# Dealing the side work of an eight-block group anew in a hybrid attention and state-space kernel

## The chip, the cores and the metric

The kernel runs on one core of one Trainium2 chip. The metric is the device time of one execution in microseconds: the median of repeated runs on the chip. The engines are named as in the profile: PE (TensorE, matrix products; PEld its weight loads), DVE (VectorE), ACT (ScalarE), POOL (GpSimd) and SP (the queue that issues the DMAs).

## The reference, cut to what matters

A layer of four parts on x of 4 x 256 rows and 512 columns: attention, a gated feed-forward, a state-space mixer, the feed-forward again. The change touches the mixer alone:

```
proj = layernorm(x) @ in_proj_w.T            # gate 8192 | x 8192, B 1024, C 1024 | dt 128
xBC  = silu(conv1d(xBC, 4 taps) + conv_b)    # each channel for itself, causal
y    = ssd(x, A, B, C, D, dt)                # 128 heads of 64, 8 groups; scores C.B^T times decay
g    = y * silu(gate)
g    = g * rsqrt(mean(g*g over a group's 1024 channels) + eps) * norm_w
x    = x + g @ out_w.T                       # 8192 channels back to 512
```

The state-space sum is computed as attention: within each sequence, the scores C·Bᵀ of a group are multiplied by every head's decay matrix and its step sizes, and then by x.

## The kernel before, in words

All matrix products of weights are made from split operands: a float32 matrix becomes a high part (ACT copies it to the float32r type) and a low part (DVE or POOL subtracts; `split`, L105 to L108), and `mm3` (L110 to L117) adds three products of 128x512 for each of four slices of the inner dimension. A projection of 128 channels for all 1024 rows is thus 24 matmuls of 128x512, in two halves of 12.

The mixer's 8192 channels are 64 blocks of 128 (two heads each), in eight groups of eight (NB = 64, GB = 8, G = 8). The function `block(i, ...)` (L1175) emits one block; `gi` is its place in the group, 0 to 7, `g` the group:

- x is projected (L1187), convolved (`conv`, L961: a bias and first tap on ACT, L964, three taps on DVE, L971, SiLU on ACT, L975) and later transposed on PE and multiplied by the step sizes (`turned`, L1022: `trx`, then `xd` on DVE).
- the gate is projected (L1208) and goes through SiLU on ACT into `gt` (L1210). A projection's PSUM comes from a pool of two (`pp`), so each waits until the one two before it has been read.
- the decay matrices of its two heads are built from DMA'd rows `r` (L996): clipped differences on DVE (L1004), a causal mask on POOL (L1008, affine select), exponentials on ACT (L1013 to L1016), and a product with the group's masked scores on DVE (L1020). Result: `em`.
- one block later, `inner_products` (L1160) makes the head products on PE (`pyy`, L1044), adds the skip and gates on DVE (L1054, L1057), stores the block to DRAM (`spill`, L1059) and adds its squares on POOL (L1067).

Beside this, each group has side work, dealt over its blocks:

- B and C of the next group: a projection and a convolution each, emitted at the end of blocks 5 and 6 (`NEXT`, L36 and L1218). In block 0 of the next group, `scores` (L978) turns them into the masked scores `gm`, eight small matmuls for each half of two projections. The convolved B and C share a tag of three buffers, `gb`, with the gated blocks.
- the out product of the group before: eight row tiles of 128 (`outer`, L1150), each 24 matmuls of 128x512 (`pog`) and one DVE addition to x (L1115). `PER` (L1174) says how many tiles each block takes: two in block 2, one each in 1 and 3 to 7. The gated blocks are recalled from DRAM at the end of the block before (`recall`, L1097, two halves a tile, two landing buffers `gr`, three split pairs `gh`), split on ACT and DVE.
- the out weights: eight loads of 256 KB a group (`out_weights`, L1073), each scaled by norm_w into a high part on ACT (L1079) and a low part on DVE (L1080). There are eight buffers, so the weights of a group can be written only after the last out product of the group before. Four are emitted in block 7 ahead of its gate, four at its end.

In blocks 0 and 1 (`late`, L1190) the head products of the block before, and the out tiles, are placed between the halves of the gate projection; in the other blocks the first out tile, the head products and the other out tiles stand between x and gate.

The next weights are fetched and split ahead: a projection prepares those of the next two in the order of the list `order` (`prepare`, L813, called at L1129 and L1130). The split's low part is made on POOL for the first 18 of them, on DVE for the rest (L819). The same `order` fixes how the weights lie in DRAM (L1303).

The framework schedules the instructions: each engine's order is fixed when the program is built, by priorities and a model of the engines, and need not be the written order. PE is the exception from group 1 on, where it keeps the written order (`manual_schedule`, L1233). Loads marked `keep_in_program_order` also stay where they are written.

After block 63 come the last head products (L1236), the out product of group 7 tile by tile with the second feed-forward, and the stores.

Of the kernel before, what the change touches and what calls it, by code (L numbers as in the profile page):

```python
# [27 lines left out]
H, PD, N, G = 128, 64, 128, 8  # L28
INTER = H * PD
NB = INTER // P  # L30
GB = NB // G
# [1 line left out]
FH = (NCL + C) // 2  # L33
EPS = 1e-5

NEXT = {5: "b", 6: "c"}  # L36


COLS = {}
# [40 lines left out]
def hybrid_kernel(  # L80
# [6 lines left out]
    nc = tc.nc  # L87
# [17 lines left out]
    def split(hl, v, engine=nc.vector):  # L105

        nc.scalar.copy(hl[0], v)  # L107
        engine.tensor_tensor(hl[1], v, hl[0].bitcast(F32), ALU.subtract)  # L108
# [677 lines left out]
    def mixer(feed, later):  # L786
        with ExitStack() as es, ExitStack() as inner:
# [17 lines left out]
            raws, pieces = {}, {}  # L805
            xs = [w1.tile([P, KC, NT], F32R, name=f"mx{i}") for i in range(2)]

            def fetch(i):
                if i < NW and i not in raws:
                    raws[i] = pw.tile([P, KC, P], F32, name="wr", tag="wr", bufs=3)  # L810
                    load(raws[i], win[i])

            def prepare(i):  # L813

                for n in range(i, i + 3):
                    fetch(n)
                if i < NW and i not in pieces:
                    pieces[i] = [pw.tile([P, KC, P], F32R, name=f"w{j}", tag=f"w{j}") for j in range(2)]
                    split(pieces[i], raws.pop(i), nc.gpsimd if i < 18 else nc.vector)  # L819

            def project(w, pp, cols):
                mm3(pp[:, cols], [[v[:, k, :] for v in w] for k in range(KC)],
# [155 lines left out]
            def scores(bt, ct):  # L978

                gm = p2.tile([P, B, 3, P], F32, name="gm", tag="gm", bufs=1)  # L980
                yield gm
                for b in range(B):
                    pg = ps.tile([P, 3, P], F32, name="pg", tag="m")
                    k0, k1 = bt[:, b * L : b * L + P], bt[:, b * L + P : (b + 1) * L]
                    q1 = ct[:, b * L + P : (b + 1) * L]
                    nc.tensor.matmul(
                        pg[:, 0:2, :].rearrange("p s i -> p (s i)"), k0, ct[:, b * L : (b + 1) * L],
                        start=True, stop=True,
                    )
                    nc.tensor.matmul(pg[:, 2, :], k1, q1, start=True, stop=True)  # L990
                    nc.vector.tensor_tensor(gm[:, b], pg, tri.rearrange("p (s i) -> p s i", s=3), ALU.mult)
                    yield

            def rows(h):
                r = p2.tile([P, NT], F32, name="r", tag="r", bufs=2)
                load(r, cumd[h : h + 1, :].to_broadcast([P, NT]))  # L996
                return r
# [40 lines left out]
            def product(xd, es2):  # L1038
                py = ps_y.tile([P, B, L], F32, name="pyy", tag="pyy")
                for b in range(B):  # L1040
                    for k in range(2):
                        for hh in range(2):
                            d = slice(hh * PD, (hh + 1) * PD)
                            nc.tensor.matmul(  # L1044
                                py[d, b, k * P :], xd[:, 2 * b + k, d],
                                es2[hh][:, b, 2 * k : 2 if k == 0 else 3, :].rearrange("p s i -> p (s i)"),
                                start=(k == 0), stop=(k == 1),
                            )
                return py

            def gated(n, x2, gt, py, sq):

                gb = po_.tile([P, NT], F32, name="gb", tag="gb", bufs=3)
                nc.vector.scalar_tensor_tensor(  # L1054
                    gb, x2, dh[:, n : n + 1], py.rearrange("p b t -> p (b t)"), ALU.mult, ALU.add
                )
                nc.vector.tensor_tensor(gb, gb, gt, ALU.mult)  # L1057
                if n < NB - 1:
                    load(spill[(n // GB) % 2][n % GB], gb)  # L1059
                else:  # L1060
                    last.append(gb)
                if sq is None:
                    sq = p2.tile([P, NT], F32, name="sq", tag="sq")
                    nc.scalar.activation(sq, gb, AF.Square)
                else:
                    nc.scalar.activation(x2, gb, AF.Square)  # L1066
                    (nc.gpsimd if n < NB - 1 else nc.vector).tensor_tensor(sq, sq, x2, ALU.add)  # L1067
                return sq
# [4 lines left out]
            def out_weights(g, k):  # L1073

                r = po_.tile([P, C], F32, name="wor", tag="wor", bufs=2)
                tc.keep_in_program_order(load(r, wout[g * GB + k]))
                n = g * GB + k
                w = [po_.tile([P, C], F32R, name=f"wo{j}", tag=f"wo{j}", bufs=GB) for j in range(2)]
                nc.scalar.activation(w[0], r, AF.Copy, scale=nw_s[:, n : n + 1])  # L1079
                nc.vector.scalar_tensor_tensor(  # L1080
                    w[1], r, nw_s[:, n : n + 1], w[0].bitcast(F32), ALU.mult, ALU.subtract
                )
                return w
# [36 lines left out]
            order = [("b", 0), ("c", 0)]  # L1120
            for n in range(NB):
                order += [("x", n), ("g", n)]
                if n % GB in NEXT and n // GB + 1 < G:
                    order.append((NEXT[n % GB], n // GB + 1))
            at = {v: i for i, v in enumerate(order)}
# [34 lines left out]
            def inner_products(m):  # L1160
                px2, gt, xd, em = stage.pop(m)
                py = product(xd, em)
                sqs[m // GB] = gated(m, px2, gt, py, sqs.get(m // GB))
# [7 lines left out]
            rr = {h: rows(h) for h in range(2)}  # L1171
            stage, sqs, wos, rgs, todo = {}, {}, {}, {}, []
            recalled = []
            PER = {1: 1, 2: 2, 3: 1, 4: 1, 5: 1, 6: 1, 7: 1}  # L1174
            def block(i, scoring, gm):  # L1175
                g, gi = divmod(i, GB)
                if gi == 0 and g:
                    scoring = scores(group["b"], group["c"])
                    gm = next(scoring)
                    todo.extend((g - 1, t) for t in range(TT))  # L1180

                def scored():

                    for _ in range(2 if gi == 0 and g else 0):
                        next(scoring)

                x2 = conv(projected("x", i, scored), i, "x2", 2)  # L1187


                late = gi < 2 and g > 0  # L1190
                if not late:
                    if recalled:
                        outer()
                    if i:
                        inner_products(i - 1)
                    while recalled:
                        outer()
                if gi == 7:
                    wos.setdefault(g, []).extend(out_weights(g, k) for k in range(4))

                def between():
                    scored()
                    if late:
                        inner_products(i - 1)
                        while recalled:
                            outer()

                pp = projected("g", i, between)  # L1208
                gt = p2.tile([P, NT], F32, name="gt", tag="gt", bufs=1)
                nc.scalar.activation(gt, pp, AF.Silu)  # L1210
                em = []
                for h in (2 * i, 2 * i + 1):
                    with tc.issue_after(silus[2]) if i == 0 else ExitStack():
                        em.append(differences(h, rr.pop(h)))
                    if h + 2 < H:
                        rr[h + 2] = rows(h + 2)
                xd = turned(i, x2)
                if gi in NEXT and g + 1 < G:  # L1218
                    convolved(NEXT[gi], g + 1)
                for e in em:  # L1220
                    weighted(e, gm)
                stage[i] = (x2, gt, xd, em)
                for _ in range(PER.get(gi + 1, 0)):
                    if todo:
                        q, t = todo.pop(0)
                        recalled.append((q, t, [recall(q, t, half) for half in range(2)]))
                if gi == 7:
                    wos[g].extend(out_weights(g, k) for k in range(4, 8))
                return scoring, gm

            for i in range(GB):
# [1 line left out]
            with tc.manual_schedule(engines={nc.tensor.engine}):  # L1233
                for i in range(GB, NB):
                    scoring, gm = block(i, scoring, gm)
            inner_products(NB - 1)  # L1236
            es_p.close()
            ps_o = pool("m_o", 4, space=PSUM, **freed)
            pos = {}
# [51 lines left out]
def arrange(inputs):  # L1291
# [12 lines left out]
    for n in range(NB):  # L1304
        order += [NB + n, n]
        g, gi = divmod(n, GB)
        if g + 1 < G and gi in NEXT:
            order.append(2 * NB + (0 if NEXT[gi] == "b" else G) + g + 1)
    blocks = wi[: (2 * NB + 2 * G) * P].reshape(-1, P, KC, P)[order]
# [48 lines left out]
```

## Time and profile before

| | us |
|---|---|
| median of 3 runs | 1892.4 (1890.96 to 1893.69) |
| profiled execution | 1894.86 |
| its span | 1893.1 |
| PE idle, 430 to 545 us (blocks 1 to 7 of group 0) | 3.7 |
| PE idle, 545 to 1800 us (groups 1 to 7) | 20.2 |
| PE idle, 1798 to 1893 us (the end) | 12.8 |

The granted TensorE clock was 0.986 over the span. "Busy" of PE is modelled from pipelined matmuls: a 128x512 matmul is shown with 390 ns, while the next starts 227 ns after it. The other engines' durations are real. A line of the timeline has start (us), duration (us), engine, line, operation, output and inputs, and a count; a bracket gives idle time ahead and what ended it. A line of waits reads: who, for whom, us in total, times, longest.

The windows used below run from one block's gate SiLU (L1210) to the next. In groups 1 to 6 such a window is 19.2 to 20.5 us where one out tile stands in it, about 24 us with B or C besides, 29 to 30 us in block 2 with its two tiles.

### The profile page before, as it was taken

The numbers are of one execution on the slowest core, as the hardware profiler recorded it, in microseconds if no ns is written. First come the engines' busy times: TensorE is split into PE (matmuls) and PEld (weight loads), VectorE is DVE, ScalarE is ACT, GpSimd is POOL, SyncE is SP. The second block draws the span as 40 slices with busy tenths as digits, with TensorE's granted clock in tenths as the row PEclk, the third lists the DMA queues.
The fourth block names the chain that finished last, engine by engine and source line by source line (L and its number), as shares of the span: only waits on it lengthen the run. The fifth ranks groups of instructions, "written<-read, shape, count | busy, mean of one in ns | idle before, by whom it ended". The sixth has DMA issues, their size and how long they took to land.

```text
span 1893.1 us, 29893 instructions
## 1 busy us (share of the span) xinstructions
PE 1812.1 (96%) x10706; PEld 1454.0 (77%) x10706; DVE 1488.3 (79%) x2304; ACT 1479.3 (78%) x2897; POOL 396.4 (21%) x393
## 2 busy tenths in 40 slices
PE   8999988899999999999999999999999999999997
PEld 6777767677777887878778877887887778777876
DVE  5566667788998788878887888778888878887767
ACT  5666675379988888978988888889788978798754
POOL 6322230014411111111212112111211212111100
PEclk8999999899999999999999999999999999999999
DMA  4000000134545445544554445445545544454241
GB/s 143 1 1 1 22 15 16 34 98 157 190 163 177 143 148 163 176 151 145 172 164 148 150 151 173 159 146 164 161 150 167 162 151 145 164 169 152 95 141 49
DMA packets 152773, 240.35 MB, mean 127 GB/s; under 512 B 12464, under 2 KB 77616, under 8 KB 152624
## 3 DMA queue, kind: packets, MB, share of 16 engines
q1 hardware_dynamic: 152624, 238.44, 39.0%
q8 instruction: 84, 1.38, 0.3%
q14 instruction: 65, 0.53, 0.1%
HBM read 202.75 MB, written 35.65 MB: 126 GB/s over the span
## 4 chain that ended last, share of the span: by engine, by line
ACT 34%; PE 25%; DVE 23%; issue 10%; DMA 6%; POOL 2%; SPq 0%; ACTq 0%; DVEq 0%; POOLq 0%
DVE acc L971 9%; ACT em L1013 4%; ACT em L1016 3%; ACT L1210 3%; ACT L1013 3%; ACT em L1014 2%; PE pp L115 2%; PE pp L116 2%; PE pp L117 2%; DVE gh L108 2%; ACT L1016 2%; ACT gt L1210 2%; ACT acc L964 2%; DMA gr<-spill 2%; ACT e L477 2%
## 5 line engine op out<-in xcount | busy, mean ns | idle before, releaser
L115 PE MATMUL pp<-mx,w 128*128 128x512 f32 (+1 forms) x1160 | 464.7, 401 | 10.1 <-ACT gt L1210 7.4
L117 PE MATMUL pp<-mx,w 128*128 128x512 f32 (+1 forms) x1160 | 452.1, 390 | 0.0
L116 PE MATMUL pp<-mx,w 128*128 128x512 f32 (+1 forms) x1160 | 451.9, 390 | 0.0
L1020 DVE TENSOR_TENSOR em<-em,gm 128x1536 f32<-128x1536 f32 x128 | 243.1, 1900 | 110.3 <-ACT em L1016 104.7
L971 DVE SCALAR_TENSOR_TENSOR acc<-pp,cw_s,acc 128x1012 f32<-128x1012 f32 (+2 forms) x240 | 303.7, 1270 | 32.5 <-ACT acc L964 29.1
L1008 POOL TENSOR_SCALAR_AFFINE_SELECT r<-r 128x512 f32<-128x512 f32 x128 | 103.4, 807 | 797.3 <-DMA r<-cumd 648.3
L115 PEld LDWEIGHTS pp<-mx,w 128*128 128x128 f32 x1160 | 218.5, 188 | 64.2 <-ACT gt L1210 11.4
L117 PEld LDWEIGHTS pp<-mx,w 128*128 128x128 f32 x1160 | 218.4, 188 | 46.6 <-issue 0.7
L116 PEld LDWEIGHTS pp<-mx,w 128*128 128x128 f32 x1160 | 218.9, 189 | 40.6 <-issue 0.6
L1067 POOL TENSOR_TENSOR sq<-sq,acc 128x1024 f32<-128x1024 f32 x55 | 151.7, 2759 | 306.3 <-ACT acc L1066 306.3
L115 PE MATMUL pog<-wo,gh 128*128 128x512 f32 x512 | 202.3, 395 | 3.2 <-DVE xd L1030 1.1
L117 PE MATMUL pog<-wo,gh 128*128 128x512 f32 x512 | 200.2, 391 | 2.5 <-DVE gh L108 2.5
L116 PE MATMUL pog<-wo,gh 128*128 128x512 f32 x512 | 199.8, 390 | 0.3 <-DVE wo L1080 0.3
L1044 PE MATMUL pyy<-em,xd 128*64 128x128 f32 (+1 forms) x2048 | 183.7, 329 | 1.3 <-DVE em L1020 1.0
L1013 ACT ACTIVATE em<-r,col_t 128x128 f32<-128x128 f32 x512 | 169.0, 390 | 9.4 <-PE pyy L1044 8.6
L1044 PEld LDWEIGHTS pyy<-em,xd 128*64 128x64 f32 x2048 | 130.1, 137 | 59.9 <-issue 18.0
L1016 ACT ACTIVATE em<-r,col_t 128x128 f32<-128x128 f32 x512 | 170.9, 390 | 0.5
L975 ACT ACT_TABLE_LOAD x65 | 83.4, 1283 | 85.3 <-DVE acc L971 85.0
L1004 DVE TENSOR_SCALAR em<-r,col_t 128x128 f32<-128x128 f32 x512 | 138.0, 324 | 7.0 <-DMA r<-cumd 5.1
L108 DVE TENSOR_TENSOR w<-wr,w 128x512 fp32r<-128x512 f32 x126 | 104.8, 831 | 34.9 <-ACT w L107 32.8
L477 ACT ACTIVATE e<-sc,nmx 128x256 f32<-128x256 f32 (+1 forms) x256 | 104.0, 441 | 21.1 <-DVE nmx L471 21.0
L115 PEld LDWEIGHTS pog<-wo,gh 128*128 128x128 f32 x512 | 96.1, 188 | 27.3 <-DVE xd L1030 2.7
(290 smaller groups left out, 3316.3 us busy)
## 6 DMA issues: line engine op xcount, KB each, us to landing
wr<-in_win_dram SPq DMA_DIRECT2D x287, 256.0 KB, 2.8
r<-cumd SPq DMA_DIRECT2D x128, 512.0 KB, 4.1
spill<-gb SPq DMA_DIRECT2D x63, 512.0 KB, 2.8
gr<-spill SPq DMA_DIRECT2D x120, 256.0 KB, 3.0
wor<-in_wout_dram SPq DMA_DIRECT2D x64, 256.0 KB, 3.2
out_dram<-x SPq DMA_DIRECT2D x8, 256.0 KB, 2.3
x<-in_x_dram SPq DMA_DIRECT2D x1, 1536.0 KB, 8.8
gr<-spill SPq DMA_DIRECT2D x8, 192.0 KB, 2.5
```

Source lines behind the costliest of these rows:

```text
L108: engine.tensor_tensor(hl[1], v, hl[0].bitcast(F32), ALU.subtract)
L115: nc.tensor.matmul(o, lh, rh, start=(first and k == 0), stop=False)
L116: nc.tensor.matmul(o, lh, rl, start=False, stop=False)
L117: nc.tensor.matmul(o, ll, rh, start=False, stop=(last and k == n - 1))
L477: nc.scalar.activation(es_[c][:, 2 * j + pr, :], sc[:, j, :], AF.Exp, bias=nm[:, j : j + 1], accum_out=rs[:, c, h : h + 1],)
L971: nc.vector.scalar_tensor_tensor(av[:, :, d:], pv[:, :, : L - d], cw_s[:, ch, tap : tap + 1], av[:, :, d:], ALU.mult, ALU.add,)
L1004: nc.vector.tensor_scalar(e[:, b, 2, :], rv[:, b, 1, :], col_t[:, h, b, 1:2], 0.0, ALU.subtract, ALU.min,)
L1013: nc.scalar.activation(e[:, b, 1, :], rv[:, b, 1, :], AF.Exp, bias=col_t[:, h, b, 2:3])
L1016: nc.scalar.activation(e[:, b, 0, :], rv[:, b, 0, :], AF.Exp, bias=col_t[:, h, b, 0:1])
L1020: nc.vector.tensor_tensor(e, e, gm, ALU.mult)
L1044: nc.tensor.matmul(py[d, b, k * P :], xd[:, 2 * b + k, d], es2[hh][:, b, 2 * k : 2 if k == 0 else 3, :].rearrange("p s i -> p (s i)"), sta ...
L1067: (nc.gpsimd if n < NB - 1 else nc.vector).tensor_tensor(sq, sq, x2, ALU.add)
```

## The change

Six edits, all in how the side work is dealt:

```
-NEXT = {5: "b", 6: "c"}
+NEXT = {3: "b", 4: "c"}
...
-                    split(pieces[i], raws.pop(i), nc.gpsimd if i < 18 else nc.vector)
+                    split(pieces[i], raws.pop(i), nc.gpsimd if i < 18 or order[i][1] % GB in (7, 0) else nc.vector)
...
-            PER = {1: 1, 2: 2, 3: 1, 4: 1, 5: 1, 6: 1, 7: 1}
+            PER = {1: 1, 2: 2, 3: 1, 4: 1, 5: 2, 6: 1}
...
-                late = gi < 2 and g > 0
+                late = gi in (7, 0, 1) and g > 0
...
-                if gi == 7:
-                    wos.setdefault(g, []).extend(out_weights(g, k) for k in range(4))
+                if gi == 6:
+                    wos.setdefault(g, []).extend(out_weights(g, k) for k in range(3))
...
                 if gi == 7:
-                    wos[g].extend(out_weights(g, k) for k in range(4, 8))
+                    wos[g].extend(out_weights(g, k) for k in range(3, 6))
+                if gi == 0 and g:
+                    wos[g - 1].extend(out_weights(g - 1, k) for k in range(6, 8))
                 return scoring, gm
...
             inner_products(NB - 1)
+            wos[G - 1].extend(out_weights(G - 1, k) for k in range(6, 8))
```

B and C of the next group come behind blocks 3 and 4. The eight out tiles are spread over blocks 1 to 6, two in blocks 2 and 5, none in 7. Block 7's head products move between the halves of its gate projection. The out weights are emitted in three parts: three in block 6 ahead of its gate, three at the end of block 7, two at the end of block 0 of the next group (of the last group: after its last head products). And the low parts of the x and gate weights of blocks 7 and 0 of every group are made on POOL; for B and C, the index is the group's number, so those of group 7 go to POOL too.

The number of instructions and of bytes is the same, but for the engine of these splits.

## The prediction

> **What bounds the kernel now.** I read the page first, then TensorE's waits in the group loop, then busy time in windows (whole loop; group boundaries; single blocks), last the ACT, DVE and POOL timelines at one boundary.
>
> ```profile
> span 1893.1 us, 29893 instructions
> ...
> PE 1812.1 (96%) x10706; PEld 1454.0 (77%) x10706; DVE 1488.3 (79%) x2304; ACT 1479.3 (78%) x2897; POOL 396.4 (21%) x393
> ```
>
> TensorE is busy for 96% of the span. The Trainium skill ("Perfetto Trace Analysis", Identifying the Most-Contended Engine) warns that matmul busy time says little and to take the weight loads' share: 77%, some 23% of room. The trace decides otherwise: in the timeline 128x512 matmuls start every 0.227 us for whole stretches, behind weight loads of 0.19 us, so the room is not there. What can be won is TensorE's idle time:
>
> ```profile
> 430.00:545.00 115.00, 111.31 (x627) 86.32 (x622) 107.66 (x132) 108.67 (x194) 48.28 (x32) 1.00 0.52 170
> 545.00:1800.00 1255.00, 1234.76 (x6774) 992.59 (x6776) 1027.54 (x1369) 1057.34 (x1785) 222.76 (x159) 1.00 0.48 156
> ```
>
> (Columns: us, busy PE, PEld, DVE, ACT, POOL, granted clock, DMA.) 3.7 us idle in group 0 and 20.2 in groups 1 to 7: 24 us in all. Where it lies, by seven windows from one group's last gate SiLU to that of block 1 of the next:
>
> ```profile
> 1268.50:1311.00 42.50, 40.65 (x236) 32.72 (x235) 36.67 (x49) 37.96 (x59) 6.36 (x4) 1.00 0.52 166
> ...
> sum 299.30, PE 283.91 PEld 227.56 DVE 257.59 ACT 266.65 POOL 49.16; mean PE 40.56 PEld 32.51 DVE 36.80 ACT 38.09 POOL 7.02
> ```
>
> 299.30 - 283.91 = 15.4 us, two thirds of the 24, lie at the seven boundaries, 2.2 us each. TensorE's waits name the causes:
>
> ```profile
> PE pp L115 <- ACT gt L1210: 7.4, 8, 1.1
> PE trx L1027 <- ACT acc L975: 5.6, 7, 1.3
> PE pog L117 <- DVE gh L108: 2.5, 6, 0.5
> ```
>
> Block 0's transposes wait for the convolved x (its SiLU), the next x projection for the PSUM that block 0's gate SiLU frees. Both are late because ACT does this in block 0:
>
> ```profile
> 1269.45 1.32 ACT L1079 ACTIVATE wo<-wor,nw_s 128x512 fp32r<-128x512 f32 x2
> ...
> 1275.95 1.19 ACT L964 ACTIVATE acc<-pp,cb_s,cw_s 128x1024 f32<-128x1024 f32 x1
> ...
> 1284.11 1.06 ACT L975 ACTIVATE acc<-acc 128x1024 f32<-128x1024 f32 x1
> 1285.08 1.36 ACT L1079 ACTIVATE wo<-wor,nw_s 128x512 fp32r<-128x512 f32 x2
> ...
> 1291.81 1.02 ACT L1210 ACTIVATE gt<-pp 128x1024 f32<-128x1024 f32 x1
> ```
>
> All eight out weights run between 1269.4 and 1286.4, although half are written ahead of block 7's gate: they fall on block 0, the one block with no out product.
>
> **Part 1: loads of the two light blocks.** After the change block 7 has no out product (24 x 0.227 = 5.4 us less on TensorE) and no C projection behind block 6. It is then like a block of group 0, whose splits are on POOL:
>
> ```profile
> 470.30:484.30 14.00, 14.00 (x82) 10.84 (x81) 13.96 (x18) 13.51 (x27) 7.57 (x5) 1.00 0.57 192
> 484.30:498.90 14.60, 14.60 (x85) 11.29 (x84) 14.17 (x18) 13.70 (x27) 7.91 (x6) 1.00 0.61 200
> ...
> 1244.20:1268.50 24.30, 24.30 (x132) 19.68 (x131) 19.46 (x26) 19.02 (x32) 3.66 (x3) 1.00 0.47 151
> 1268.50:1286.30 17.80, 17.05 (x103) 13.77 (x102) 14.30 (x18) 15.28 (x26) 1.27 (x2) 1.00 0.66 204
> ```
>
> Such a block takes TensorE 14.0 to 14.6 us, with DVE and ACT nearly full and no wait: good news and a warning. DVE of block 7 now: 19.46, less C's convolution and split (3 x 1.27 + 0.69) and the tile's add (0.74), is 14.2 for a bare block. Now: block 7 fits (19.5 in 24.3); block 0 needs 14.2 + 4 x 0.55 (masked scores) + 8 x 0.77 (weights) = 22.5 against 17.05 of TensorE work: 5.5 us behind, of which 2.2 become TensorE waits and 3.3 are absorbed. After: block 7 needs 14.2 - 2 x 0.69 (splits to POOL) + 3 x 0.77 = 15.1 against 14.6; block 0 14.2 + 2.2 + 3 x 0.77 = 18.7 against 17.05; together 2.2 us behind, less than the 3.3 absorbed. Weights 6 and 7 (1.5 us of DVE, 1.4 of ACT) come behind block 0's gate, in block 1 with its out product, and are needed there only after x, half the gate and the block's product. ACT drops five weights (5 x 0.71) ahead of block 0's gate, so its 1.1 us wait goes too. I leave 0.3 us per boundary: 7 x 0.3 - 15.4 = -13.3 us (ends: -15.4, and 0 if the weights bunch again).
>
> **Part 2: a new wait in block 7.** With no out product, from the end of x to the transposes TensorE has only the gate projection and the product: 5.6 + 2.8 = 8.4 us (now 14). In that time ACT and DVE must do bias, three taps, table load and SiLU: in group 0's light blocks 8.2 us (bias at 489.77, SiLU over at 497.9), in block 0 above 9.2 behind a start 1.1 late, in block 4 9.6 behind 3.8. So 0 to 5 us a group. I take 0.5: order and load are group 0's, plus some of three weights. 7 x 0.5 = +3.5. The product's move between the gate's halves (late) costs TensorE nothing and gives the decay products 2.8 us more; without that, they would be due 5.7 us after block 6's transposes, about when they are ready now (1180.65, 5.5 after 1175.2).
>
> **Part 3: splits to POOL.** Four a group (x and gate of blocks 7 and 0), and B and C of group 7 by their index. The Trainium skill ("SBUF — State Buffer", Who interferes with whom) speaks against it: DVE operations with two SBUF inputs and POOL lock one port pair, and the later blocks wholly. The trace, POOL first, then DVE:
>
> ```profile
> 474.99 3.98 POOL L108 TENSOR_TENSOR w<-wr,w 128x512 fp32r<-128x512 f32 x2 [0.75 <-ACT w L107]
> ```
> ```profile
> 443.14 4.50 DVE L1020 TENSOR_TENSOR em<-em,gm 128x1536 f32<-128x1536 f32 x2
> ...
> 474.83 1.75 DVE L1020 TENSOR_TENSOR em<-em,gm 128x1536 f32<-128x1536 f32 x1
> ```
>
> A split takes 2.0 us there. At 474.8 DVE lost nothing beside it; at 443.1, beside two, 4.50 - 2 x 1.75 = 1.0. By the rule four splits block up to 8 us of DVE and save 2.8, and the backlog of 2.2 would exceed 3.3; by the rows they block 0 to 2 and save 2.8. I take the rows, with the gain in part 1. POOL's queue: a split can stand behind an affine select that waits for its rows' DMA; group 0 has the same queue and no wait for it, and a split is called for two projections (over 10 us) ahead.
>
> **Part 4: heavier blocks 3 to 5.** B and C behind 3 and 4, two tiles in 5. DVE in blocks 3 and 4 is 15 to 16 of 20 us; plus 4.5 against 5.4 of TensorE it still fits. B and C hold two of three gb buffers for two blocks more; a gated block gives the third back after its spill (2.8 us), so 0, at most 2.8 a block if the cover goes. Two tiles recalled together need four gh pairs with three there: SP then waits on gr behind DVE, and spills, rows and weights queue behind it. Block 2 does this already, with waits of 0.5 us six times on the late DVE; that shrinks with the backlog and comes back once in block 5. I put the two at 0 (-2.5 to +3.5).
>
> **Part 5: ends.** In group 0 blocks 6 and 7 both become light, with three weights in each: +0.7 (0 to +3). In the last group the weights come earlier; TensorE now waits 1.4 us for them after 1800 (1.1 on ACT, 0.3 on DVE). Two remain late, hidden under four tiles' first halves: -1.2 (0 to -1.5).
>
> Sum: -13.3 + 3.5 + 0.7 - 1.2 = -10.3 us. The profiled execution took 1894.9 us (span 1893.1 and 1.8 around it), 2.5 above the median of the runs; applied to the median, 1892.4 - 10.3 = 1882.
>
> **Rivals.** (a) All waits go: block 7 runs as group 0's light blocks do, 0 there and 0 at the boundary: -15.4 - 2.5 - 1.2 = -19: 1873, and 1867 were all 24 us of the loop to go. For it: the 14.0 us rows. Against it: DVE full before any weight is added. (b) Slower: the x chain of block 7 takes the place of the wait removed. At block 4's 3.8 + 9.6 against 8.4 it costs 5.0 a group, 7 x 5.0 - 13.8 = +21: 1913; at 3 us, +7: 1900. It decides from about 2.0 us a group. For it: ACT starts most convolutions late, and DVE, in order, puts other work between the taps. Against: those blocks' transposes aren't due earlier. (c) The backlog only moves: ACT and DVE still run the weights in one burst in block 0, since operations are not placed where they are written (now they ran 10 us later), or POOL blocks DVE as the rule says. Then the change doesn't do what it says, and gains at most the tail: 1891.
>
> **How the numbers follow.** Likeliest 0.53 (1874 to 1888); (a) 0.13; (b) 0.18, half of it under 1900; (c) 0.16. A measurement tells about 0.2% from no change, 3.8 us. Faster: 0.53 + 0.13 = 0.66; same, (c): 0.16; slower, (b): 0.18. The range, 1868 to 1897, covers all but half of (b) and a tenth at both edges.
>
> **What would show it.** Right: weight scalings in three places, no wait of the transposes in block 0, boundary windows with under 0.6 us of idle TensorE, that of blocks 6 to 7 short by 5 to 11 us and those of 3 to 5 longer. Wrong: transposes of block 7 waiting over 2 us on the SiLU (b); the eight weights still in one run, or DVE's two-input operations stretched beside POOL's splits (c); a new wait on gh in block 5.

## The result, and the profile after

The changed kernel takes 1892.4 us (median of 12 runs, 1889.28 to 1894.44), the kernel before 1891.3 (12 runs beside them). The ratio is 1.0009, with a 95% interval of 0.9999 to 1.002: no difference that these runs can tell. The profiled execution took 1893.5 us, and these are its span, its busy times, and the windows that the prediction used for its idle time (us, busy PE, PEld, DVE, ACT, POOL, granted clock, DMA share, GB/s):

```profile
span 1891.7 us, 29927 instructions
...
PE 1806.6 (96%) x10706; PEld 1454.4 (77%) x10706; DVE 1503.3 (79%) x2272; ACT 1425.3 (75%) x2851; POOL 459.7 (24%) x425
```
```profile
430.00:545.00 115.00, 108.56 (x608) 84.61 (x607) 108.66 (x126) 108.44 (x187) 54.06 (x33) 1.00 0.56 175
545.00:1800.00 1255.00, 1232.10 (x6765) 993.15 (x6764) 1041.10 (x1341) 1002.00 (x1741) 278.62 (x188) 1.00 0.48 156
```

TensorE's idle time in the loop is not smaller: 6.4 us in group 0 (3.7 before) and 22.9 in groups 1 to 7 (20.2 before). Between 545 and 1800 us ACT lost 55 us of work: the framework, with its new order of ACT's operations, sets 188 loads of a function table (1.28 us each) in place of 235, so the number of instructions is not quite the same. POOL took 56 us more. DVE's busy time rose by 13.6 us, although 27 splits left it. Its operations ran longer: the clipped differences (L1004) took 363 ns on average against 305, the decay products (L1020) 2009 against 1912. An estimate from the two traces, each operation against the shortest tenth of its kind, puts 71 us of such lengthening beside POOL's squares (L1067), against 52 before, and 2 us beside POOL's splits. TensorE has nothing from all this. Its idle time has moved, though. Its waits between 430 and 1800 us (us in total, times, longest):

```profile
PE trx L1027 <- ACT acc L975: 20.7, 11, 3.0
PE pp L115 <- DVE acc L971: 3.0, 2, 1.7
PE trx L1027 <- DVE x L1115: 2.6, 6, 0.4
```

The wait for block 0's gate SiLU (7.4 us) is gone, and so is that for the split pairs `gh` (2.5). The wait of the transposes for x's SiLU has grown from 5.6 to 20.7 us. Where it lies is told by two sets of windows of the changed kernel. The first runs, in groups 1 to 6 (the groups are 0 to 7), from block 6's gate SiLU to block 7's (last line of each: the sums):

```profile
887.50:905.70 18.20, 16.30 (x95) 12.80 (x94) 15.11 (x20) 15.16 (x29) 4.19 (x4) 1.00 0.58 191
1067.80:1085.10 17.30, 15.32 (x91) 11.97 (x90) 14.51 (x18) 15.11 (x28) 4.79 (x4) 1.00 0.59 187
...
sum 106.30, PE 92.67 PEld 72.67 DVE 88.12 ACT 90.44 POOL 27.93; mean PE 15.45 PEld 12.11 DVE 14.69 ACT 15.07 POOL 4.66
```

and the second from there to the gate SiLU of block 1 of the next group, the boundary windows of the prediction:

```profile
1266.70:1307.60 40.90, 39.34 (x228) 31.47 (x227) 35.88 (x49) 34.85 (x56) 10.24 (x5) 1.00 0.48 162
...
sum 242.90, PE 236.93 PEld 190.23 DVE 213.97 ACT 209.14 POOL 62.26; mean PE 39.49 PEld 31.71 DVE 35.66 ACT 34.86 POOL 10.38
```

The boundary waits went down from 2.2 us each to (242.90 - 236.93) / 6 = 1.0, and block 7, which had none, now has (106.30 - 92.67) / 6 = 2.3. From the first gate SiLU of the mixer to the last the changed kernel takes 1390.5 us, against 1386.2 before (+4.3); from there to the end 91.1 against 94.3 (-3.2); and it reaches the first one 2.5 us earlier, in a stretch that the change doesn't touch.

Block 7 of group 4 shows the new wait. On ACT (an operation's start and duration; the bracket gives idle time ahead and what ended it):

```profile
1255.49 0.72 ACT L1079 ACTIVATE wo<-wor,nw_s 128x512 fp32r<-128x512 f32 x1 [0.99 <-DMA wor<-in_wout_dram]
1256.13 1.19 ACT L964 ACTIVATE acc<-pp,cb_s,cw_s 128x1024 f32<-128x1024 f32 x1
...
1262.87 1.28 ACT L975 ACT_TABLE_LOAD   x1 [0.40 <-DVE acc L971]
1264.16 1.06 ACT L975 ACTIVATE acc<-acc 128x1024 f32<-128x1024 f32 x1
```

on DVE, and on TensorE:

```profile
1257.35 2.59 DVE L971 SCALAR_TENSOR_TENSOR acc<-pp,cw_s,acc 128x1012 f32<-128x1012 f32 x2 [0.34 <-ACT acc L964]
1259.85 1.75 DVE L1020 TENSOR_TENSOR em<-em,gm 128x1536 f32<-128x1536 f32 x1
1261.52 1.27 DVE L971 SCALAR_TENSOR_TENSOR acc<-pp,cw_s,acc 128x1020 f32<-128x1020 f32 x1
```
```profile
1265.27 0.98 PE L1027 MATMUL trx<-con,acc 128*128 128x128 f32 x7 [2.06 <-ACT acc L975]
```

From the start of the bias (L964) to the end of the SiLU (L975) it is 1265.2 - 1256.1 = 9.1 us, and the bias starts over 1 us behind the end of x. TensorE has work for 8.4 us from the end of x. Two things stand in the chain that needn't: a decay product of 1.75 us between the second and the third tap, and the third out weight ahead of the bias, for whose DMA ACT waited 0.99 us. The same order stands in groups 1 to 6. The weights no longer run in one burst: in this group ACT scales them at 1250.4 (two), 1255.5, 1265.1, 1267.6, 1272.7 and 1294.1 (two), where before all eight ran between 1269.4 and 1286.4.

### The profile page after: what moved, and what is told of

Read it like the earlier page. It is cut to its first block, busy times and chain, and to the rows that moved or that the text cites. A ratio compares the mean times of both kernels' runs of the same rounds, so it can differ in the third digit from the quotient of the medians.

```text
span 1891.7 us, 29927 instructions
## 1 busy us (share of the span) xinstructions
PE 1806.6 (96%) x10706; PEld 1454.4 (77%) x10706; DVE 1503.3 (79%) x2272; ACT 1425.3 (75%) x2851; POOL 459.7 (24%) x425
## 4 chain that ended last, share of the span: by engine, by line
PE 61%; ACT 14%; DVE 13%; DMA 4%; issue 4%; POOL 3%; SPq 0%; DVEq 0%; ACTq 0%; POOLq 0%
PE pp L115 8%; PE pp L116 8%; PE pp L117 8%; PE pyy L1044 6%; PE pog L115 6%; PE pog L116 6%; PE pog L117 6%; DVE acc L971 3%; DMA wor<-in_wout_dram 2%; ACT e L477 2%; PE trx L1027 2%; DVE em L1020 1%; POOL sq L1067 1%; ACT em L1016 1%; ACT em L1013 1%
## 5 line engine op out<-in xcount | busy, mean ns | idle before, releaser
L1020 DVE TENSOR_TENSOR em<-em,gm 128x1536 f32<-128x1536 f32 x128 | 254.6, 1992 | 40.1 <-ACT em L1016 40.1
L1008 POOL TENSOR_SCALAR_AFFINE_SELECT r<-r 128x512 f32<-128x512 f32 x128 | 127.2, 995 | 629.3 <-DMA r<-cumd 488.8
L1067 POOL TENSOR_TENSOR sq<-sq,acc 128x1024 f32<-128x1024 f32 x55 | 149.7, 2722 | 355.1 <-ACT acc L1066 355.1
L1004 DVE TENSOR_SCALAR em<-r,col_t 128x128 f32<-128x128 f32 x512 | 168.1, 383 | 28.3 <-PE pyy L1044 22.2
L1044 PE MATMUL pyy<-em,xd 128*64 128x256 f32 (+1 forms) x2048 | 183.4, 330 | 0.8 <-DVE em L1020 0.8
L107 ACT CAST w<-wr 128x512 fp32r<-128x512 f32 x144 | 88.4, 614 | 83.2 <-PE pp L116 79.6
L107 ACT CAST gh<-gr 128x512 fp32r<-128x512 f32 (+1 forms) x128 | 76.5, 607 | 52.8 <-PE pog L116 42.4
L115 PEld LDWEIGHTS pog<-wo,gh 128*128 128x128 f32 x512 | 96.1, 188 | 22.9 <-issue 3.8
```

Source lines behind the costliest of these rows:

```text
L115: nc.tensor.matmul(o, lh, rh, start=(first and k == 0), stop=False)
L1004: nc.vector.tensor_scalar(e[:, b, 2, :], rv[:, b, 1, :], col_t[:, h, b, 1:2], 0.0, ALU.subtract, ALU.min,)
L1020: nc.vector.tensor_tensor(e, e, gm, ALU.mult)
L1044: nc.tensor.matmul(py[d, b, k * P :], xd[:, 2 * b + k, d], es2[hh][:, b, 2 * k : 2 if k == 0 else 3, :].rearrange("p s i -> p (s i)"), sta ...
```

## The experiments

My theory after the result (T): the spread weights do shorten the boundaries, as forecast; but without its out tile block 7 gives the x chain only 8.4 us, and the chain, with other work in its way, needs over 10. So one wait replaces the other. Rivals: POOL's splits slow DVE (P); the heavier blocks 3 to 5, or the weights' two landing buffers, are the cause. Every kernel was timed in five rounds beside the kernel before; the ratios below are to that, with 95% intervals.

### One part undone: splits back on DVE

```
-split(pieces[i], raws.pop(i), nc.gpsimd if i < 18 or order[i][1] % GB in (7, 0) else nc.vector)
+split(pieces[i], raws.pop(i), nc.gpsimd if i < 18 else nc.vector)
```

> The changed kernel with the split's low part back on DVE after group 0 (the POOL edit undone, all else kept). Theory T (the wait of block 7's transposes for the convolved x, 2.1 to 3.2 us a group, eats the gain; its cause is that TensorE's way from x to transposes is 8.4 us with no out tile, and ACT and DVE take 10.4): the wait in block 7 stays at 2 us or grows by up to 0.7; 1890 to 1898 us. Rival P (POOL and DVE block each other[...], and that makes the taps late): the wait of block 7 falls below 1 us, 1880 to 1886 us.

Measured: 1913.5 us, ratio 1.0115 (1.0096 to 1.0134). Slower by about 20 us, which neither side had expected: P is refuted, and T was far too low. In block 7 of group 4 ACT, ahead of the bias:

```profile
1266.70 0.72 ACT L1079 ACTIVATE wo<-wor,nw_s 128x512 fp32r<-128x512 f32 x1 [2.68 <-DMA wor<-in_wout_dram]
1267.32 1.19 ACT L964 ACTIVATE acc<-pp,cb_s,cw_s 128x1024 f32<-128x1024 f32 x1
```

The 2.68 us are the longest wait of its kind: over groups 1 to 6 ACT waits 1.5 us on average for the third weight's DMA, against 1.2 in the changed kernel. Besides, a split of 0.68 us stands between the taps. Together they make block 7's wait 3.1 us, against 2.3. That is about 5 us of the 20 with group 7. The rest lies elsewhere; TensorE's three largest waits between 430 and 1800:

```profile
PE trx L1027 <- ACT acc L975: 18.9, 7, 4.2
PE pog L117 <- DVE gh L108: 6.9, 6, 1.2
PE pp L115 <- ACT gt L1211: 3.6, 5, 1.0
```

Block 2's out product waits again for the split pairs `gh`, made late on DVE (6.9 us, none in the changed kernel), and block 1's x projection for block 0's gate SiLU (3.6 in all, against 0.6). Only block 0's own wait for the SiLU, 3.6 us in the changed kernel, is gone. So the splits cost time in several places where DVE is late; the 20 us were not taken apart further. SP's queue is not shown to be the way: at the loads of weights (L811) it stood 190.5 us for DVE's splits between 545 and 1800, and in the changed kernel 133.4 for DVE's and 60.9 for POOL's, as much together.

### The tile back in block 7

The changed kernel with `PER` and `late` as before and the first three weights in block 7, behind its out tile.

> The changed kernel with one out tile back in block 7 (the list of tiles and the late placement as before the change), so that weights 0 to 2 come in block 7 behind that tile, 3 to 5 at its end, 6 and 7 at the end of block 0; B and C behind 3 and 4 and the POOL splits kept. Theory T: no wait of block 7's transposes (TensorE has 14 us from x to transposes); block 0 keeps a wait of about 1 us; 1876 to 1885 us. Rival W (the weights' place decides, wherever the tile is): waits of 2 us per group stay, 1888 to 1895 us.

Measured: 1882.9 us, ratio 0.9953 (0.9935 to 0.9971), 10 us faster than with the tile away. Block 7 has no wait from group 1 on. For the SiLU 10.0 us of waits remain, 2.3 in group 0's block 7 and the rest in block 0, and 4.7 for block 1's step products. The weights' first place and the place of block 7's head products went back with the tile, so this is the tile with what belongs to it.

### The x chain of block 7 freed

Two pins, by `issue_after`, which fixes an order on one engine: in block 7 the decay products stand behind the last tap on DVE (`tap`); in the first kernel the three out weights also stand behind x's SiLU on ACT (`silu`). Tiles, weights and splits are as in the changed kernel.

```
+                with tc.issue_after(tap) if gi == 7 else ExitStack():
                     for e in em:
                         weighted(e, gm)
...
-                if gi == 6:
-                    wos.setdefault(g, []).extend(out_weights(g, k) for k in range(3))
+                if gi == 7:
+                    with tc.issue_after(silu):
+                        wos.setdefault(g, []).extend(out_weights(g, k) for k in range(3))
```

Both:

> The changed kernel with two orders fixed in block 7: on DVE the decay products of that block behind the last tap of its convolution, and on ACT weights 0 to 2 behind the SiLU of its x. Theory T in its finer form (of the 10.4 us from x to SiLU, 1.3 is a weight in ACT's way that waits for its DMA, and 1.75 a decay product between the taps on DVE): the wait in block 7 falls to 0 to 0.5 us; weights then meet in block 0, which keeps or adds up to 1 us; 1878 to 1888 us. Rival F (ACT and DVE are full over blocks 7 and 0, so that order doesn't matter): the wait moves to block 0 whole, 1890 to 1896 us.

Measured: 1880.8 us, ratio 0.9944 (0.9926 to 0.9962). Only the decay products:

> The changed kernel with only the first of these orders: on DVE, block 7's decay products behind the last tap. Theory T: the wait in block 7 falls by 1.2 to 1.7 us to about 0.5 to 1; 1881 to 1888 us. Rival F: no change, 1890 to 1895 us.

Measured: 1879.3 us, ratio 0.9937 (0.9916 to 0.9958): fixing the order of one kind of operation on DVE, with what the framework then orders differently around it, is worth 13 us. The same block of group 4 in this kernel, on DVE and TensorE:

```profile
1250.07 3.90 DVE L971 SCALAR_TENSOR_TENSOR acc<-pp,cw_s,acc 128x1012 f32<-128x1012 f32 x3 [0.34 <-ACT acc L964]
...
1255.19 1.75 DVE L1020 TENSOR_TENSOR em<-em,gm 128x1536 f32<-128x1536 f32 x1
```
```profile
1257.07 1.09 PE L1027 MATMUL trx<-con,acc 128*128 128x128 f32 x8 [0.21 <-ACT acc L975]
```

The three taps run as one, the chain takes 8.2 us, and the transposes wait 0.2 in place of 2.1. All waits for x's SiLU between 430 and 1800:

```profile
PE trx L1027 <- ACT acc L975: 4.9, 13, 0.8
```

The weights alone:

> The changed kernel, but ACT runs block 7's three out weights behind the SiLU of its x (the other of the two pins; block 7's decay products stay between the taps). T: both things in the way of block 7's x chain count, the decay product between the taps with 1.75 us and the late bias with about 1.0 to 1.3; without the second the wait of 2.1 to 3.2 us falls to about 1.3 a group: 1883 to 1887 us. Rival: the bias had slack and the product between the taps is the whole of it (its removal alone gave -12 us): 1890 to 1894.

Measured: 1901.9 us, ratio 1.0068 (1.0054 to 1.0082): neither theory. With the weights away from the bias the framework dealt DVE's order anew and put block 6's skip (L1054) between the taps too:

```profile
1265.49 1.27 DVE L971 SCALAR_TENSOR_TENSOR acc<-pp,cw_s,acc 128x1012 f32<-128x1012 f32 x1 [4.30 <-ACT acc L964]
1266.67 1.75 DVE L1020 TENSOR_TENSOR em<-em,gm 128x1536 f32<-128x1536 f32 x1
1268.34 1.27 DVE L971 SCALAR_TENSOR_TENSOR acc<-pp,cw_s,acc 128x1016 f32<-128x1016 f32 x1
1269.53 1.27 DVE L1054 SCALAR_TENSOR_TENSOR gb<-acc,dh,pyy 128x1024 f32<-128x1024 f32 x1
1270.71 1.27 DVE L971 SCALAR_TENSOR_TENSOR acc<-pp,cw_s,acc 128x1020 f32<-128x1020 f32 x1
```

The chain is 10.9 us long and the transposes wait 2.85 us, with no weight and no DMA ahead of the bias. So what lies between the taps is enough to make the wait. Whether the late bias adds to it is told by the traces of all these kernels together. In groups 1 to 6 the wait of block 7's transposes is, within 0.1 us, the time for which ACT waits for the third weight's DMA, plus the time from the bias's start to the SiLU's end, less 8.02 us (taken from the changed kernel's group 4):

| kernel, group | wait for DMA | bias to SiLU | sum less 8.02 | transposes waited |
|---|---|---|---|---|
| changed, 4 | 0.99 | 9.09 | 2.06 | 2.06 |
| changed, 1 | 1.95 | 9.09 | 3.02 | 3.01 |
| splits on DVE, 4 | 2.68 | 9.56 | 4.22 | 4.21 |
| products pinned, 4 | 0.04 | 8.18 | 0.20 | 0.21 |
| weights pinned, 4 | none | 10.87 | 2.85 | 2.85 |
| both pinned, 4 | none | 7.94 | below 0 | none |

So both count, each with its full length. Of the 1.85 us that the pin of the products takes off in group 4, 0.91 are the shorter chain and 0.95 the wait for the DMA, which went although no edit aims at it; why it went stays open.

### More landing buffers

The out weights and the recalled halves share one ring of four buffers (each had two), so that a weight's load can start earlier; then the same with the decay products of blocks 7 and 0 behind the last tap.

```
-name="wor", tag="wor", bufs=2      -name="gr", tag="gr", bufs=2
+name="wor", tag="gr", bufs=4       +name="gr", tag="gr", bufs=4
```

> The changed kernel with the two landing buffers of the out weights and the two of the recalled blocks made one ring of four (same space). Theory T: in block 7 the third weight waits 0.99 us for its DMA, which waited for a landing buffer, just ahead of the bias of x on ACT; with four buffers the bias starts when x is done and the wait of block 7's transposes falls from 2.1 to about 1 us; 1882 to 1887 us. Rival F (the decay product between the taps, and full engines, set the wait): at most 0.3 us a group, 1889 to 1894 us.

Measured: 1900.1 us, ratio 1.0053 (1.0034 to 1.0072).

> The changed kernel with the ring of four landing buffers, and the decay products of blocks 7 and 0 both behind the last tap of their block's x. Theory T: gains of both add where each is on the x chain: wait of block 7 near 0, of block 0 under 0.5 us; 1870 to 1876 us. If the wait is only handed on: as with the first order alone, 1878 to 1881 us.

Measured: 1902.1 us, ratio 1.0075 (1.0058 to 1.0092). Both have lost block 7's wait for the SiLU, and their loops take 1384.7 and 1383.6 us against 1390.5. What they win there is lost at the end, 100 and 103 us against 91.1. In the first of them, after 1790,

```profile
PE pog L115 <- ACT gh L107: 7.2, 1, 7.2
```

the first out product of group 7 waits 7.2 us for a recalled half, which now lands in the ring that the last weights use: SP issued the loads of the halves from 1796.9 on, behind the last group's weights. In the second the last waits are others (6.5 us for the squares, L1067). The first one's profile is of its fastest run, 1892.4 us; where the others lose another 8 us no trace shows. A shared ring was a poor way to ask for more landing space; a buffer more for the weights alone was not tried.

### One part alone, on the kernel before

> The kernel before with only the splits of blocks 7 and 0 put on POOL. If the POOL edit is worth as much here as in the changed kernel (21 us there): 1868 to 1875 us. If it matters only where block 7 is light, because the splits are late there and hold up SP's queue: 1885 to 1891 us; I expect this, with up to 1 us less wait per boundary.

Only the splits on POOL: 1888.0 us, ratio 0.9994 (0.9984 to 1.0004). No difference.

> The kernel before with only the out weights dealt anew: three in block 7 behind its out tile, three at its end, two at the end of block 0; B, C, tiles and splits as before. If the eight weights in one run made block 0's 2.2 us of waits (step 1 of the prediction): the waits there fall by half or more, 1878 to 1885 us. If they bunch all the same (rival c): 1889 to 1893 us.

Only the weights spread (three in block 7 behind its tile, three at its end, two at the end of block 0): 1878.7 us, ratio 0.9944 (0.9927 to 0.9961). This is the forecast's main gain by itself. Waits of this kernel between 430 and 1800:

```profile
PE trx L1027 <- DVE xd L1030: 5.5, 7, 0.8
PE trx L1027 <- ACT acc L975: 3.1, 7, 1.5
```

For a gate SiLU TensorE waits 0.6 us in all (7.4 before); block 1's transposes wait for DVE in place of it.

### Two more parts undone

B and C back behind blocks 5 and 6, the rest as changed:

```
-NEXT = {3: "b", 4: "c"}
+NEXT = {5: "b", 6: "c"}
```

> The changed kernel with B and C of the next group back behind blocks 5 and 6. T: C's convolution then stands on ACT and DVE right ahead of block 7's x chain, which has only TensorE's 8.4 us: C's three taps and its split add at least 2 us of lateness to the 2.5 of wait, so 5 or more a group: 1905 to 1915 us. Rival: the heavier blocks 3 to 5 cost what the change gives, and B and C do no harm where they were: about 1880 us.

Measured: 1911.0 us, ratio 1.0113 (1.0095 to 1.013), as T expects. The same with the splits back on DVE too, so that only weights and tiles are dealt anew:

> The changed kernel with B and C back behind blocks 5 and 6 and the splits back on DVE: of the change only the spread weights and the dealing of tiles (two in block 5, none in block 7) are left. The kernel before with the spread weights alone, its tile still in block 7, took 1878.7 us. T: taking the tile out of block 7 is what the other edits have to pay for; the x chain of block 7 gets about 5.6 us less and DVE 2.8 us more work than in the changed kernel: 1910 to 1930 us. Rival: the tile's place costs nothing by itself: 1876 to 1884 us.

Measured: 1919.6 us, ratio 1.0147 (1.0128 to 1.0165), also T's. In both the size came as expected and the place did not. The largest wait of TensorE in the second (the first has the same with 17.1 us), and its place in group 4:

```profile
PE pp L115 <- DVE acc L971: 19.3, 7, 3.2
```
```profile
1264.77 0.39 PE L117 MATMUL pp<-mx,w 128*128 128x512 f32 x1
1268.18 0.77 PE L115 MATMUL pp<-mx,w 128*128 128x512 f32 x1 [3.03 <-DVE acc L971]
1268.75 0.63 PE L116 MATMUL pp<-mx,w 128*128 128x512 f32 x1
```

TensorE stops right at the end of block 7's x, ahead of the gate: of the two `pp` buffers x holds one and C's projection the other, until DVE's third tap of C has read it. With C right ahead of block 7 and no tile between x and gate, TensorE comes to that buffer 5.4 us sooner. I had looked for the price in x's own chain.

### Weights, splits and a pin, on the kernel before

The weights spread, splits on POOL, and weights 3 to 5 behind the SiLU of block 0's x (`issue_after`), instead of at the end of block 7.

> The kernel before with the out weights spread, its tile still in block 7, plus the splits of blocks 7 and 0 on POOL, and weights 3 to 5 on ACT behind the SiLU of block 0's x instead of the end of block 7. With the weights spread alone TensorE still waited 3.1 us for block 0's SiLU and 5.5 us for block 1's step products, both behind DVE. T: splits on POOL take 2.8 us a group off DVE, the pin takes two weights from between block 0's taps; most of 8.6 us goes: 1870 to 1875 us. Rival: POOL's splits stretch DVE's own work and the weights only come later, into block 1: 1877 to 1884 us.

Measured: 1878.0 us, ratio 0.9938 (0.9926 to 0.995). The two waits that it was aimed at are gone from the top of the list, yet it is no faster than the spread weights alone, and the theory's 1870 to 1875 us is missed. The largest total of waits left is 2.6 us; why the shorter waits gave no shorter time stays open.

```profile
PE trx L1027 <- DVE x L1115: 2.6, 6, 0.4
PE pg L986 <- DVE xd L1030: 1.6, 2, 1.0
```

Three versions thus lie at 1878 to 1879 us by different means, and their intervals overlap: the spread weights, that with POOL and a pin, and the changed kernel with its decay products pinned.

## Why the prediction was wrong

**What bounds the kernel**: right. TensorE's idle time of some 24 us was what could be won, two thirds of it at the boundaries; the weights alone took 10 us off the time.

**Part 1, the boundaries**: right in mechanism, too large in this setting. The weights alone changed the medians by 1878.7 - 1888.9 = -10.2 us against the forecast -13.3 (the estimate of 0.3 us left per boundary was low: block 1's transposes still wait 0.8). In the changed kernel 1.0 us is left per boundary, not 0.3.

**Part 2, the new wait in block 7**: the step that failed. The mechanism was named, with 8.4 us for TensorE and 8.2 for the chain, and then I took 0.5 us a group because "order and load are group 0's, plus some of three weights". It measured 2.3. The order isn't group 0's: from group 1 on the framework put a decay product of 1.75 us between the taps, and the third weight ahead of the bias waited for its DMA, 1.2 us on average over groups 1 to 6. By the sum of the table above the first leaves a wait of 9.09 - 8.02 = 1.07 us, and the second adds its 1.2 whole: 2.3. The trace of before could have warned of the first, since the last group's block 7 has a decay product between x's taps there too; the second came with the weights' new place. At six groups the 1.8 us by which 0.5 was too low are 11 us, the largest part of what the forecast of -10.3 lacks. The 0.7 us too little at six boundaries (4 us) and group 0 (part 5) add to it, and so does TensorE's clock, which the forecast had put at nothing: it fell to half behind three of these waits (last section), at some 1.7 us each, against one such fall before. The waits for `gh` that went take 2.5 us off. Pinning the decay products, which takes block 7's wait to 0.2, gave the forecast back: 1879.3 us in place of the 1882 forecast. Rival (b) had the mechanism and its point of balance, "about 2.0 us a group"; the measurement fell near that point, so the time is that of no change.

**Part 3, splits on POOL**: right that they do not slow DVE, wrong on what they are for. The rule of the Trainium skill ("SBUF — State Buffer", Who interferes with whom) would have had four splits block DVE for up to 8 us a group, by the prediction's estimate; alone they change nothing measurable (0.9994). The rule itself is borne out where the two meet; they seldom do. In the changed kernel, of 28 splits between 545 and 1800 us, 17 meet no DVE operation with two SBUF inputs and take 1.28 to 1.30 us. A split that begins beside such an operation with 0.57 us left to go took 1.72; two DVE operations that began beside a split with 1.09 and 1.23 us to go took 0.95 and 1.03 longer; overlaps of 0.1 us left no mark on the split. So the split of 2.0 us that I read in group 0, begun 0.16 us behind a decay product, holds a wait for it, and the 8 us were too high from the start. In the new dealing, without the tile's cover, the splits on POOL are worth about 20 us, in several waits behind DVE; I had put them at no more than the 2.8 us a group that they take off DVE.

**Part 4, the heavier blocks**: right from group 1 on. Blocks 3 to 5 show no wait there that was not there before, and the waits for `gh` (2.5 us) went rather than came back. In group 0 block 5 has a new wait of 1.7 us for a projection's buffer, behind C. Moving B and C is not a cost here but a need: with them back it is 1911 us.

**Part 5, the ends**: right in sign. Group 0 has 2.7 us more idle time, within the range of 0 to 3. The waits for out weights at the end, 1.4 us, are gone, and the end is 3.2 us shorter; block 63's transposes now wait 2.9 us, which was not seen coming.

So the expected gain was made and spent in the next block: rival (b), to which I had given 0.18, near its break-even point. Rival (c), that the weights still bunch, is refuted by their three places. That the changed kernel equals the kernel before is an accident of terms that cancel, not a sign of a change without effect.

## What to carry to other kernels

A block's cover for a latency chain is the work of the bounding engine between the chain's two ends; when a change takes such work out, compute what the chain needs with everything that the scheduler has put between its links, in that stage's own trace, not in a lighter stage that looks alike. Where a scheduler orders the engines, pin the two or three operations of the chain that became critical: one pin was worth 13 us here, the six edits together nothing. Parts of a change are not additive: the same splits on POOL were worth nothing with the cover in place and 20 us without it.

## What the runs showed that I had not expected

A wait of TensorE of 2 to 3 us can be followed by a stretch at half clock, and whether it is depends on when it begins. In the kernel with tiles and weights dealt anew only (1919.6 us), windows before, in and after such a stretch:

```profile
1264.80:1268.00 3.20, 0.36 (x2) 0.00 (x0) 3.20 (x4) 1.72 (x2) 0.00 (x0) 0.93 0.94 302
1268.00:1271.00 3.00, 2.82 (x7) 2.27 (x8) 3.00 (x4) 2.87 (x4) 0.63 (x1) 0.50 0.65 219
1271.00:1274.00 3.00, 3.00 (x27) 2.10 (x27) 2.60 (x4) 1.55 (x3) 0.00 (x0) 1.00 0.59 175
```

The granted clock is 0.50 for about 3.4 us right after the wait of 3.03, and seven matmuls run where 13 would. So such a wait costs some 1.7 us more than it lasts. In the changed kernel this followed block 7's waits of 3.0, 2.7 and 2.9 us in groups 1, 6 and 7, and not those of 1.9 to 2.1; with the weights alone pinned, it followed four of six equal waits of 2.9.

The Trainium skill ("TensorE: Matmul & The Clock Gate", Part 1: The HAM clock gate) has the clock fall after an idle window of some 3.4 us that runs freely, whenever the wait begins. The traces agree on the grid: in the changed kernel the three stretches start at 721.36, 1629.30 and 1799.97 us, 266 and 50 times 3.413 us apart. They differ on how idle the window must be. I divided all fourteen traces between 430 and 1805 us into windows of their own grid and took the time in each without a matmul. Thirty half-clock stretches begin there, each right behind a window with at least 1.85 us of idle time; of the other 5591 windows at full clock none has more than 1.93. So a little over half a window is enough, if it falls into one window. With the shared ring of landing buffers, waits of 1.92 and 1.94 us in block 0, each inside one window, were followed by half clock three times; the changed kernel's waits of 1.9 to 2.1 were split by the grid, with at most 1.70 in one window. The three fastest kernels (1878 to 1879 us) have no such stretch, the changed kernel three, by the 1.7 us each some 5 of the 13 to 14 us between them.
